# Layer 0 of a convolution and attention kernel: other weights for sharing out the depthwise taps, and an iteration's end written out by hand

## Chip, cores and metric

The kernel runs on one core of a Trainium2 chip. The metric is the device time of one execution in microseconds (us); lower is better. PE is the matrix engine, DVE the vector engine, ACT the scalar engine, POOL the general engine, SP the engine that issues the DMAs.

## What is computed

Eight images of 256 channels and 32 x 32 positions go through two layers. The change is in layer 0, which is, for each image (`_ln` scales by the root mean square over the channels):

```python
a = _attention(_ln(x, norm1_w, norm1_b), ...)
x = x + gamma1 * a
f = _edffn(_ln(x, norm2_w, norm2_b), pi_w, dw_w, fft_p, po_w)
x = x + gamma2 * f

# _attention: 4 heads, 32 channels for q and k, 64 for v
qkv = _bn(_conv1x1(x, qkv_w), ...)
attn = softmax(einsum('bhkn,bhkm->bhnm', q, k) * SCALE)
out = einsum('bhdm,bhnm->bhdn', v, attn)
out = out + _bn(_dwconv3(v_img, pe_w), ...)      # a 3x3 depthwise convolution of v
return _bn(_conv1x1(out, proj_w), ...)

# _edffn
x = _dwconv3(_conv1x1(x, pi_w), dw_w)            # 1024 channels
x = gelu(x1) * x2                                # 512 channels
x = _conv1x1(x, po_w)
# then an 8x8 Fourier filter with fft_p
```

Layer 1 (causal attention over the eight images' tokens and a mixture of eight experts) is the same before and after.

## The kernel before

Layer 0 is a software pipeline over the images, one iteration `i` per image. `main_of(i)` (L1052) is a generator that issues, in one order, the work that is mostly PE's: the second norm of image i-1 (`norm2`) and the Fourier part of image i-2 (`spectrum`: `pz`, `pf`, `py`), woven with the first attention units; the rest of the attention of image i (`attend`, L725) woven with the queries and keys of image i+1 (`queries_keys`); and then the end: copies of the queries and keys into a stacked form (`stack`, 32 DMAs on SP), the values of image i+1 (`values`, L685), the last softmax denominators (`finish`, L809), the Gelus of image i-1 (`gelu_steps`), and the output projection with its residual (`project`, L815).

An attention unit is a block of 128 keys against 256 queries: four matmuls into `s`, an exponential on ACT (`pT`), and, one unit late, the products with the values (`po`) and with ones (`sums`). Eight units make a chunk of 256 queries, four chunks an image. After a chunk, `close` copies `po` and `sums` off (`pu`, `ss`), and some units later come a reciprocal on DVE (`sr`), its split in two on ACT and POOL (`rh`, `rl`), a spreading matmul (`rb`) and two DVE operations that add the chunk to `o`. For the last chunk of an image these steps are in `finish`.

The depthwise convolutions run on DVE, one multiply-add over 128 x 1024 elements for each tap (`tap`, L537): 16 taps for the values of image i (`v_conv`, into `o`), and 8 groups of 8 taps for the hidden channels of image i-1 (`hidden`, L886, into `x` or `conv`; the ninth tap is in ACT's eviction). Each group of `hidden` first needs a 1x1 convolution on PE, `ph`, in two halves, and two ACT evictions for each half, into `hpad` (padded, two buffers) and into the accumulator. `open_group` (L843) issues them at the fourth and the sixth tap of the group before. When a group of the second half of the channels and its Gelu are done, `gate` multiplies the two (`hid`, two DVE operations), and `spectrum` of the next iteration reads `hid`. At the fourth tap of the next to last group, `hidden` asks for one Gelu itself if none has been done.

Every generator yields a weight, an estimate in us. `together` (L411) issues the side generator (`hidden`, with `v_conv` as its lead) whenever its sum of weights is below that of the main one, and what is left at the main one's end is issued after it:

```python
    for us in main:
        a += us
        while side is not None and s < ratio * a:
            step = next(side, None)
```

All of this is program order: every engine works off its own queue in the order in which the instructions were issued, and waits on semaphores. Operations go through a wrapper that keeps this order, so in the profile they all have its line, L68, and are told apart by their tiles. `ps_s` (tag `s`) and `ps_m` (tag `mm`) are PSUM pools of two buffers each; `s`, the values' `pq`, `pz` and the first half of the projection use `ps_s`, and `ph`, the queries' `pq`, `tpv`, `rb` and the second half of the projection use `ps_m`.

An attention unit has the weight 1.75 (L803), and a tap of the lead its own 1.3 times 1.5 (L898). In the end, `values` and `project` have weights of their own, so taps are given out among them too; `finish` and the Gelus are put between the steps of `values`:

```python
ends = weave(finish(i), gelu_steps(i - 1) if i >= 1 else none(), 1)
if i + 1 < B:
    stack(i + 1)
    yield from weave(values(i + 1), ends, 1)
    yield from project(i, (0, 1))
```

Of the kernel before, what the change touches and what calls it, by code (L numbers as in the profile page):

```python
# [9 lines left out]
F32 = mybir.dt.float32  # L10
F32R = mybir.dt.float32r
BF16 = mybir.dt.bfloat16
AF = mybir.ActivationFunctionType
# [5 lines left out]
P = 128  # L19
B, C, H, W = 8, 256, 32, 32  # L20
N = H * W
HALF = 512
KC = C // P
# [50 lines left out]
def conv_attn_hybrid_kernel(  # L74
# [353 lines left out]
    with ExitStack() as l0:  # L428
# [101 lines left out]
        def interior(p, h):  # L530
            r = H // 2
            return p[:, 1 + h * r : 1 + (h + 1) * r, 1 : 1 + W]

        def rows(ap):
            return ap.rearrange("p (h w) -> p h w", w=W)
# [89 lines left out]
        def conv1x1(ps, w, o0, src, hs):  # L625
            for k in range(KC):
                pe.matmul(
                    ps, w[:, k, o0 : o0 + P], src[:, k, hs], start=(k == 0), stop=(k == KC - 1)
                )


        att = {}
# [52 lines left out]
        def values(b):  # L685


            vT = att[b]["vT"] = one.tile([P, NT, C], F32, tag="vT", name="vT")
            waiting = []

            def turn(g, h, full):
                tp = ps_m.tile([P, 4, P], F32, tag="mm", name="tpv")
                for j in range(4):
                    pe.transpose(tp[:, j, :], full[:, j * P : (j + 1) * P], ident)
                act.copy(vT[:, 4 * h : 4 * h + 4, g * P : (g + 1) * P], tp)

            for g in range(KC):
                bias = qkv_o[:, 2 + g : 3 + g]
                pq = ps_s.tile([P, 2, HALF], F32, tag="s", name="pq")
                for h in range(2):  # L700
                    hs = slice(h * HALF, (h + 1) * HALF)
                    conv1x1(pq[:, h, :], qkvw, (2 + g) * P, att[b]["xn"], hs)
                for h in range(2):
                    full = one.tile([P, HALF], F32, tag="full", name="vfull", bufs=2)
                    act.activation(full, pq[:, h, :], AF.Identity, bias=bias)
                    act.activation(interior(vpad[g], h), rows(pq[:, h, :]), AF.Identity, bias=bias)
                    yield 1.7
                    if waiting:
                        turn(*waiting.pop())
                        yield 0.5  # L710
                    waiting.append((g, h, full))
            turn(*waiting.pop())
            yield 0.5

        def v_conv(b):
            o = att[b]["o"] = one.tile([P, KC, N], F32, tag="o", name="o")
# [8 lines left out]
        def attend(b):  # L725

            qst, kst, vT = (att[b][n] for n in ("qst", "kst", "vT"))
            nj = NT  # L730
            todo = []

            def product(po, sm, j, pT):


                for pair in range(NH // 2):
                    for i in range(4):
                        ch = pair * P + i * KD
                        pe.matmul(
                            po[i * KD : (i + 1) * KD, pair, :],  # L740
                            vT[:, j, ch : ch + KD],
                            pT[:, ch // HD, :],
                            start=(j == 0 and pair == 0),
                            stop=(j == nj - 1 and pair == 1),
                        )
                for hd in range(NH):
                    pe.matmul(
                        sm[hd * KD : (hd + 1) * KD, :], ones[:, :KD], pT[:, hd, :], start=(j == 0), stop=(j == nj - 1)
                    )

            def close(c, po, sm):
                pu = two.tile([P, NH // 2, QC], F32, tag="pu", name="pu", bufs=1)
                act.copy(pu, po)
                ss = two.tile([P, QC], F32, tag="ss", name="ss", bufs=1)
                act.activation(ss, sm, AF.Copy, accum_out=accs[:, 0, b, c : c + 1])
                r = two.tile([P, QC], F32, tag="sr", name="sr", bufs=1)
                rh = two.tile([P, QC], F32R, tag="rh", name="rh", bufs=1)
                rl = two.tile([P, QC], F32R, tag="rl", name="rl", bufs=1)
                qs = slice(c * QC, (c + 1) * QC)

                def invert():
                    dve.reciprocal(r, ss)

                def split():
                    act.activation(rh, r, AF.Copy, accum_out=accs[:, 1, b, c : c + 1])
                    pool.tensor_sub(rl, r, rh.bitcast(F32))

                def spread():
                    rb = ps_m.tile([P, NH // 2, QC], F32, tag="mm", name="rb")
                    for pair in range(NH // 2):  # L770
                        pe.matmul(rb[:, pair, :], pick_r[:, pair, :], rh, start=True, stop=False)
                        pe.matmul(rb[:, pair, :], pick_r[:, pair, :], rl, start=False, stop=True)
                    o = att[b]["o"][:, :, qs]
                    dve.tensor_mul(pu, pu, rb)
                    dve.tensor_add(o, o, pu)

                return [None, invert, None, split, None, None, spread]

            def later():
                if todo:  # L780
                    step = todo.pop(0)
                    if step:
                        step()

            late = None
            for c in range(N // QC):
                qs = slice(c * QC, (c + 1) * QC)
                po = ps_o.tile([P, NH // 2, QC], F32, tag="po", name="po")
                sm = ps_o.tile([P, QC], F32, tag="sm", name="sums")
                for j in range(nj):  # L790
                    ks = slice(j * P, (j + 1) * P)
                    s = ps_s.tile([P, NH, QC], F32, tag="s", name="s")
                    for hd in range(NH):
                        pe.matmul(s[:, hd, :], kst[:, hd, ks], qst[:, hd, qs], start=True, stop=True)
                    pT = two.tile([P, NH, QC], F32, tag="pT", name="pT")
                    act.activation(pT, s, AF.Exp)
                    if late:
                        product(*late[:4])
                        if late[2] == nj - 1:
                            todo = close(c - 1, *late[:2])  # L800
                    late = (po, sm, j, pT)
                    later()
                    yield 1.75  # L803
            product(*late)
            todo = close(c, po, sm)
            att[b]["rest"] = todo
            yield 1.3

        def finish(b):  # L809
            for step in att[b]["rest"]:  # L810
                if step:
                    step()
                yield 0.4
# [72 lines left out]
        def hidden(b, lead, on_pe=(), alone=False):  # L886
# [4 lines left out]
            for i, us in enumerate(lead):  # L891
                if i == 14:
                    opening = open_group(b, 0, hpad[0])
                    cur = next(opening)
                if i in (14, 15):
                    next(opening)

                yield 1.5 * us  # L898
            if opening is None:
                opening = open_group(b, 0, hpad[0])  # L900
                cur = next(opening)
# [131 lines left out]
        def weave(main, side, every, rest=True):  # L1033

            for n, us in enumerate(main):
                yield us
                if n % every == every - 1:
                    step = next(side, None)
                    if step is not None:
                        yield step  # L1040
            if rest:
                yield from side

        def none():
            yield from ()

        def later_on(n, steps):
            for _ in range(n):
                yield 0.0
            yield from steps  # L1050

        def main_of(i):  # L1052

            steps = attend(i)
            if i >= 1:
                head = weave(norm2(i - 1), spectrum(i - 2) if i >= 2 else none(), 1)
                yield from weave(head, steps, 3, rest=False)  # L1060
            later = queries_keys(i + 1) if i + 1 < B else none()
            yield from weave(steps, later_on(2, weave(set_up(), later, 1) if i == 0 else later), 2)
            ends = weave(finish(i), gelu_steps(i - 1) if i >= 1 else none(), 1)
            if i + 1 < B:
                stack(i + 1)
                yield from weave(values(i + 1), ends, 1)
                yield from project(i, (0, 1))
            else:
                yield from weave(project(i, (0,)), ends, 1)
                yield from project(i, (1,))  # L1070


# [22 lines left out]
        nc.vector.tensor_mul(proj_o, proj_o, cols("gam1"))  # L1095
        for _ in steps:
            pass
        for _ in values(0):
            pass
        ng = HID // P  # L1100
        dw_w = cols("dw_w").rearrange("p (g k) -> p g k", k=9)
        pi_o = const.tile([P, 2 * ng], F32, name="pi_o")
# [445 lines left out]
    with ExitStack() as l2:  # L1548
# [235 lines left out]
        for n in range(len(pieces) + LAG3):  # L1784
            one_ = two_ = three = iter(())
            if n < len(pieces):
                h, b, e = pieces[n]
                i = n // NE
# [141 lines left out]
```

## Time and profile before

| | |
|---|---|
| median of 3 runs | 3302.47 us (3299.11 to 3310.37) |
| the profiled execution | 3301.58 us, span 3299.8 us |
| busy: PE, DVE, ACT, POOL | 3061.8 (93%), 2415.3 (73%), 1424.7 (43%), 308.4 (9%) us |
| attention units (`pT` on ACT, 256 of them) | from 46.3 to 1236.1 us, so layer 0 is roughly the first 1290 us |
| taps of the hidden channels and of the values | 1.28 to 1.30 us each |
| span of one iteration, images 2 to 6 | 160.8 us |

The profile is one execution; times in it count from its first instruction. A row of the timeline has the start, the time, the engine, the operation with its output and inputs, how many, and in brackets the idle time of that engine before it and what ended it. A 32-bit matmul shows as two records (`pp` x16 are eight instructions). A row of the table of windows has a stretch, its length, the busy time and the instructions of each engine in it, and the clock that PE was granted (PEclk, 1.00 is full).

### The profile page before, as it was taken

The page shows a single profiled execution, that of the slowest core. Times are in us where ns is not written, and L with a number is a line of the kernel's source. Part 1 is how long each engine was busy: PE and PEld are TensorE (multiplying, and loading weights), DVE is VectorE, ACT ScalarE, POOL GpSimd, SP SyncE. Part 2 cuts the span into 40 slices and gives each one's busy share as a digit, 9 for nine tenths or more (in the row PEclk, how much of TensorE's full clock was granted, in tenths as well). Part 3 has the DMA queues.
Part 4 walks back from the last instruction along what each step waited for, and adds up shares of the span by engine and source line. Part 5 has one row for each costly group of instructions (what it writes and reads, how often), then busy time and mean ns, then how long its engine had stood idle before and what let it go on. Part 6 is the DMA issues. An engine that isn't in the chain of part 4 may idle for free.

```text
span 3299.8 us, 43136 instructions
## 1 busy us (share of the span) xinstructions
PE 3061.8 (93%) x17218; PEld 2058.1 (62%) x17218; DVE 2415.3 (73%) x3796; ACT 1424.7 (43%) x2215; POOL 308.4 (9%) x472
## 2 busy tenths in 40 slices
PE   8997999999999996769999998999999999999999
PEld 4553555555555553346565665677878777777787
DVE  4378787878787876835555444588888878888887
ACT  4454455555555552323333332344444444444443
POOL 2100211111111100011222211000000000000000
PEclk9998999999999998889999999899999999999999
DMA  3202020202020200030111101200000000000000
GB/s 110 52 2 51 27 52 27 52 27 52 27 52 27 52 19 2 16 135 26 63 63 53 39 26 52 94 20 20 20 20 20 24 22 26 20 20 26 20 7 13
DMA packets 49831, 121.45 MB, mean 37 GB/s; under 512 B 7302, under 2 KB 20054, under 8 KB 45782
## 3 DMA queue, kind: packets, MB, share of 16 engines
q1 hardware_dynamic: 49622, 118.61, 11.4%
q8 instruction: 137, 2.24, 0.3%
q14 instruction: 72, 0.59, 0.1%
HBM read 48.20 MB, written 37.88 MB: 26 GB/s over the span
## 4 chain that ended last, share of the span: by engine, by line
PE 48%; DVE 5%; ACT 1%; POOL 1%; issue 1%; DMA 0%; SPq 0%; POOLq 0%; ACTq 0%; DVEq 0%
PE pm L68 12%; PE pa L68 12%; PE q L68 11%; PE s L68 4%; PE po L68 3%; PE pv L68 2%; PE pk L68 2%; DVE nm L68 1%; DVE pr L68 1%; DVE zt L68 1%; DVE st L68 1%; ACT pr L68 1%; PE tp L68 1%; DVE h L68 1%; PE tpz L68 1%
## 5 line engine op out<-in xcount | busy, mean ns | idle before, releaser
L68 ACT ACTIVATE h<-h,bn_o,bn_s 128x512 f32<-128x512 f32 x384 | 308.6, 813 | 628.5 <-DVE h L68 628.4
L68 DVE SCALAR_TENSOR_TENSOR conv<-hpad,vec,conv 128x1024 f32<-128x1024 f32 x256 | 330.5, 1296 | 14.1 <-ACT conv L68 8.3
L68 DVE SCALAR_TENSOR_TENSOR x<-hpad,vec,x 128x1024 f32<-128x1024 f32 x248 | 320.0, 1295 | 26.3 <-ACT x L68 20.5
L68 PE MATMUL pm<-h,w 128*128 128x512 f32 (+1 forms) x768 | 323.4, 530 | 0.0
L68 ACT ACTIVATE pT<-s 128x1024 f32<-128x1024 f32 x256 | 261.4, 1023 | 135.2 <-PE s L68 134.5
L68 PE MATMUL po<-pT,vT 128*32 128x256 f32 x4096 | 276.4, 388 | 6.9 <-ACT pT L68 6.4
L68 PE MATMUL ph<-xn,piw 128*128 128x512 f32 x512 | 250.2, 617 | 6.9 <-DVE t L68 3.9
L68 PE MATMUL s<-kk,z 128*128 128x512 f32 x512 | 244.7, 606 | 0.6 <-DVE pr L68 0.6
L68 PE MATMUL s<-qst,kst 128*128 128x256 f32 x1024 | 212.5, 330 | 0.0
L68 PEld LDWEIGHTS s<-qst,kst 128*128 128x128 f32 x1024 | 145.6, 191 | 87.4 <-issue 81.2
L68 PEld LDWEIGHTS pm<-h,w 128*128 128x128 f32 x768 | 147.7, 192 | 77.1 <-issue 63.4
L68 ACT ACTIVATE hpad<-ph,pi_o 128x512 f32<-128x512 f32 x126 | 87.1, 691 | 250.0 <-PE ph L68 225.8
L68 DVE TENSOR_TENSOR h<-pa,first 128x512 f32<-128x512 f32 x128 | 88.3, 690 | 138.2 <-PE pa L68 136.5
L68 DVE TENSOR_TENSOR h<-h,wb 128x1024 f32<-128x1024 f32 x128 | 156.3, 1221 | 41.0 <-ACT h L68 41.0
L68 PE MATMUL pz<-pow__117,hid 128*128 128x256 f32 x512 | 131.3, 410 | 55.7 <-DVE hid L68 55.7
L68 DVE SCALAR_TENSOR_TENSOR o<-vpad,pe_w,o 128x1024 f32<-128x1024 f32 x128 | 163.3, 1280 | 14.5 <-ACT o L68 11.6
L68 DVE TENSOR_TENSOR h<-h,first 128x256 f32<-128x256 f32 x384 | 163.2, 425 | 13.2
L68 PEld LDWEIGHTS po<-pT,vT 128*32 128x32 f32 x4096 | 107.4, 109 | 90.8 <-ACT pT L68 8.1
L68 PEld LDWEIGHTS ph<-xn,piw 128*128 128x128 f32 x512 | 91.1, 192 | 116.2 <-issue 92.8
L68 PE MATMUL pa<-tz,ws 128*128 128x256 f32 x512 | 156.1, 387 | 3.0 <-DMA ws<-sums_d 3.0
L68 PE MATMUL sums<-pT,ones 128*32 128x256 f32 x2048 | 158.8, 382 | 0.0
L68 PE MATMUL q<-t,ws 128*128 128x256 f32 x512 | 152.7, 380 | 0.8 <-DVE t L68 0.8
(279 smaller groups left out, 5853.6 us busy)
## 6 DMA issues: line engine op xcount, KB each, us to landing
td<-t SPq DMA_DIRECT2D x8, 1024.0 KB, 3.8
t<-td SPq DMA_DIRECT2D x8, 1024.0 KB, 4.8
te<-ud SPq DMA_DIRECT2D x16, 512.0 KB, 3.9
out_dram<-te SPq DMA_DIRECT2D x16, 512.0 KB, 2.8
ze<-zd SPq DMA_DIRECT2D x15, 512.0 KB, 3.9
t<-in_x_dram SPq DMA_DIRECT2D x7, 1024.0 KB, 6.3
qst<-hi SPq DMA_DIRECT2D x56, 128.0 KB, 2.3
qst<-lo SPq DMA_DIRECT2D x56, 128.0 KB, 2.3
```

Source lines behind the costliest of these rows:

```text
L68: return self._tc.keep_in_program_order(method(*args, **kwargs))
```

## The change

An attention unit has the weight 2.4 and a tap of the lead 1.3 times 1.7. The end of all iterations but the last is a new generator, `ending`, whose steps have no weight, so that no tap is issued between them. Its order is: first half of the values' matmuls (`product(0)`), the reciprocal of the last chunk, a Gelu, evictions (`take(0)`), the second half's matmuls, the split of the reciprocal, a Gelu, the transposes of the first half (`turn`), the first half of the projection, the evictions of the second half, a Gelu, the spreading of the reciprocals, the second transposes, and the second half of the projection. `values` returns its three pieces for this in place of being a generator; before the first iteration they are called in the order product, take, turn, turn. The last iteration keeps its end, and its calls are the same.

```diff
@@ values @@
-            waiting = []
-
-            def turn(g, h, full):
+            pqs, fulls = {}, {}
+
+            def product(g):
+                pq = pqs[g] = ps_s.tile([P, 2, HALF], F32, tag="s", name="pq")
+                for h in range(2):
+                    conv1x1(pq[:, h, :], qkvw, (2 + g) * P, att[b]["xn"], slice(h * HALF, (h + 1) * HALF))
+
+            def take(g):
+                bias = qkv_o[:, 2 + g : 3 + g]
+                for h in range(2):
+                    full = fulls[g, h] = one.tile([P, HALF], F32, tag="full", name="vfull", bufs=2)
+                    act.activation(full, pqs[g][:, h, :], AF.Identity, bias=bias)
+                    act.activation(interior(vpad[g], h), rows(pqs[g][:, h, :]), AF.Identity, bias=bias)
+
+            def turn(g, h):
                 tp = ps_m.tile([P, 4, P], F32, tag="mm", name="tpv")
+                full = fulls.pop((g, h))
...
+            return product, take, turn
@@ attend @@
-                    yield 1.75
+                    yield 2.4
@@ hidden @@
-                yield 1.5 * us
+                yield 1.7 * us
@@ new @@
+        def ending(i):
+            product, take, turn = values(i + 1)
+            gelus = gelu_steps(i - 1) if i >= 1 else none()
+            rest = finish(i)
+            product(0)
+            yield 0.0
+            next(rest)
+            next(rest)
+            next(gelus, None)
+            take(0)
+            product(1)
+            yield 0.0
+            next(rest)
+            next(rest)
+            next(gelus, None)
+            for h in range(2):
+                turn(0, h)
+                yield 0.0
+            for _ in project(i, (0,)):
+                yield 0.0
+            take(1)
+            next(gelus, None)
+            for _ in rest:
+                pass
+            for h in range(2):
+                turn(1, h)
+                yield 0.0
+            for _ in gelus:
+                pass
+            for _ in project(i, (1,)):
+                yield 0.0
@@ main_of @@
-            ends = weave(finish(i), gelu_steps(i - 1) if i >= 1 else none(), 1)
             if i + 1 < B:
                 stack(i + 1)
-                yield from weave(values(i + 1), ends, 1)
-                yield from project(i, (0, 1))
+                yield from ending(i)
             else:
-                yield from weave(project(i, (0,)), ends, 1)
+                yield from weave(project(i, (0,)), weave(finish(i), gelu_steps(i - 1), 1), 1)
                 yield from project(i, (1,))
@@ before the loop @@
-        for _ in values(0):
-            pass
+        product, take, turn = values(0)
+        for g in range(KC):
+            product(g)
+            take(g)
+            for h in range(2):
+                turn(g, h)
```

More of the change, by code (lines that the diff above doesn't have):

```diff
@@ L695, in turn @@
                 act.copy(vT[:, 4 * h : 4 * h + 4, g * P : (g + 1) * P], tp)
[L697 to L713, printed above, removed]
+            return product, take, turn
         def v_conv(b):
```

## The prediction

> **What bounds the kernel now.** I read the page first (PE is busy for 93% of the span, and the longest pieces of the chain of waits are PE matmuls), then the table of windows. The change touches only layer 0, the first 1290 us. There, images 2 to 6 repeat every 160.8 us, so I cut one of these iterations (image 5) into its first part, its attention part and its end, and add the ends of images 7, 1 and 0:
>
> ```profile
> core 0: us, PE busy (x) PEld busy (x) DVE busy (x) ACT busy (x) POOL busy (x), PEclk, DMA share, GB/s
> 799.80:844.10 44.30, 42.74 (x298) 28.48 (x298) 38.60 (x44) 19.80 (x29) 8.84 (x14) 1.00 0.01 1
> 844.10:932.80 88.70, 85.81 (x857) 46.70 (x855) 70.98 (x62) 50.94 (x78) 14.01 (x17) 1.00 0.10 33
> 932.80:960.60 27.80, 23.37 (x61) 11.09 (x62) 25.10 (x25) 15.65 (x26) 0.84 (x1) 0.88 0.54 124
> 1237.60:1287.50 49.90, 24.12 (x60) 11.85 (x60) 42.90 (x42) 12.76 (x20) 1.06 (x1) 0.73 0.01 2
> 262.60:292.50 29.90, 25.45 (x72) 11.77 (x68) 24.70 (x24) 18.23 (x30) 0.93 (x1) 0.94 0.57 130
> 292.50:321.40 28.90, 11.06 (x28) 6.18 (x32) 28.29 (x27) 6.01 (x8) 0.00 (x0) 0.70 0.00 0
> 131.00:153.00 22.00, 19.15 (x81) 8.93 (x84) 6.05 (x8) 10.18 (x21) 0.72 (x1) 1.00 0.76 175
> ```
>
> The attention part is PE's: 85.8 of 88.7 us, while DVE is idle for 17.7. In the end it is the reverse: DVE 25.1 of 27.8, PE waiting, and its granted clock at 0.88. The last image is the extreme: 49.9 us with PE busy for half. Next, the timeline of PE in that end of image 5, and of its `pp` in image 0's end for comparison (start, us, engine, what, idle before):
>
> ```profile
> 944.57 0.66 PE L68 MATMUL tpv<-ident,vfull 128*128 128x128 f32 x4 [0.40 <-ACT vfull L68]
> 947.15 0.65 PE L68 MATMUL tpv<-ident,vfull 128*128 128x128 f32 x4 [1.93 <-ACT vfull L68]
> 949.56 0.58 PE L68 MATMUL rb<-rh,pick_r 128*128 128x256 f32 x1 [1.75 <-ACT rh L68]
> 951.29 9.33 PE L68 MATMUL pp<-o,projw 128*128 128x512 f32 x16
> ```
> ```profile
> 145.93 7.03 PE L68 MATMUL pp<-o,projw 128*128 128x512 f32 x16
> ```
>
> Two waits of 1.9 and 1.75 us, and then a projection of 9.33 us that takes 7.03 elsewhere (part of the 2.3 may be its second half's wait for `o`). Last, what DVE waits for in the attention part (total, times, longest):
>
> ```profile
> DVE pu L68 <- PE rb L68: 5.3, 2, 4.1
> DVE xn L68 <- PE rbn L68: 4.4, 1, 4.4
> DVE lo L68 <- ACT hi L68: 4.2, 2, 3.3
> DVE sr L68 <- ACT ss L68: 2.0, 2, 1.3
> ```
>
> DVE is ahead there: its taps have been given out too thinly for the time PE takes, and it stands at the next result of PE or ACT.
>
> [...] 0.88 in the end, after 3.7 us of idling within 4.9 us, and 1.00 in the attention part with gaps up to 1.1; (1-0.88) of 27.8 us is 3.3 us of PE's clock lost. [...] the `sr` of the end stands behind every tap given out before it (944.6, twelve us after `sums`). [...] The trace has 1.28 us, with the Gelu 0.01 us behind it; I use 1.28.
>
> **The change part by part.** *How many taps move.* Weights up to the start of the end, images 2 to 6: attention 32x1.75+1.3 = 57.3, `norm2` 6.4, `spectrum` 21.2, `queries_keys` 13.2, sum 98.1. The first 16 taps cost 1.3x1.5 = 1.95 each, the other 64 1.3, so 68 of 80 are given out and 12 are left (the window shows 14, DVE being two behind). Now attention is 78.1, the sum 118.9, and the taps cost 16x2.21+64x1.3 = 118.6: none is left. Image 1 (no `spectrum`) reaches 97.7, that is 64 taps instead of 52; image 7 (no `queries_keys`) 71 instead of 58. So the change doesn't do what it says in images 1 and 7, where 16 and 2 taps still come behind the projection.
>
> *Attention part, images 2 to 6.* 14 taps at 1.30 us (18.22 us in the window) come in: DVE 70.98+18.2 = 89.2 us. With them come two halves of `ph` at 1.72 = 3.4 us of PE. The first Gelu moves into attention, because the next to last group asks for one at its fourth tap: the order on ACT shows a table load, the Gelu, two half groups' evictions, and a table load back before the next `pT`. The pair of loads and the Gelu is 2x1.28+1.06 = 3.6 us of ACT; PE has 5.2 us of `ph` and `pq` beside it but only two `mm` buffers, so `pT` and with it `po` come late by between 0 and 3.6; taken 2.0. One us more for further half groups ahead of a `pT` (0 to 2; today's waits of this kind are 0.8 to 1.1 each). PE: 88.7+3.4+2.0+1.0 = 95.1. DVE has 89.2 of work in it, so 5.9 us may be lost to the waits above instead of 17.7; DVE may also run some three taps late before a `hpad` write on ACT stops, which is why I take it as covered.
>
> *The end.* From the end of `sums`, by the order listed and the durations of the trace. PE: `pq` 3.4+3.4, eight `tpv` to 8.0, first half of `pp` 3.5 to 11.5, `rb` 0.6 to 12.1, four `tpv` to 12.6. ACT: `pu`, `ss`, table, Gelu to 3.5; the first four evictions 3.7 to 6.0; `rh`, Gelu to 7.6; `vT` to 8.9; four evictions to 11.2; Gelu to 12.2. So the first `tpv`, `pp` and `rb` wait for nothing. DVE has no tap: `t` of the first half to 12.4, `hid` to 13.7, `pu` and `o` to 15.1. PE's last `tpv` need the buffer that `pu` frees (14.5), the second half of `pp` needs `o`: 15.3 to 18.8. I take 19.2 for 27.8, at full clock, the longest gap being 1.9. Bounds: 17.7 (no gap) and 22.5 (3.3 us of half clock come back).
>
> *First part.* The 0.7 us that `pz` waits for the last `hid` goes: 43.6 for 44.3. SP's queue: the 32 copies of `stack` take 20.2 us and 2.3 to land from the last `s` on; the next `s` comes some 26 us after that instead of 37, still behind them. POOL has one `rl`. Hidden, at nothing.
>
> Per image: 43.6+95.1+19.2 = 157.9 against 160.8, -2.9; five images -14.5.
>
> *Image 7.* Attention part +6.9 (four halves of `ph`), +2 (tables), +0.5. Then DVE: today 36.7 us of its 42.9 behind `sums` are taps (31.5) and gates; now nine taps (11.8), the gates (5.2), `sr`, `pu`, `o` and `t` (5.9) make 23 us, and with some 4 of waits for Gelu and projection the last `hid` is about 27 us after `sums`, not 46.4. Sum 9.4+27-46.4 = -10 (-5 to -13). *Image 1:* 109.6+6.9+1 in its first part, 19.5 for 29.9, then 16 taps, gates and `pz` 29.5 for 28.9, since PE has nothing else: -2. *Image 0:* its end, without Gelus, is 20.1 today: -1. *Prologue:* the second `pq` now waits behind `tpv` that wait for ACT: +1. Each of these three may be 3 off to either side.
>
> Sum: -14.5-10-2-1+1 = -26.5. The profiled execution took 3301.6 (span 3299.8 and 1.8 around it), 0.9 under the median; so about 3275 there, and **3276** as a median.
>
> **Rivals.** (a) *The clock returns, nothing is gained.* If the gap before the second `pp` pushes PE to half clock in each end as now (3.3 us lost), and the table loads cost all of their 3.6 us, the five images give 5x(-2.9+3.3+1.6) = +10 in place of -14.5, so 3300. For it: today's ends fall to half clock on gaps of this size. Against: today two of them stand in a row, and the end as worked out has one. (b) *DVE becomes the bound, slower.* In the attention part DVE's 89.2 us meet a window of 95.1. It decides from 5.9 us of DVE waits on. If the 15.9 us listed above all stayed, an image would take 10.0 more: 5x(-2.9+10.0) = +35.5, less 12 in the other images: about 3326. For it: DVE at 94%, and every late `xn`, `lo`, `pu` holds a `pq` or `mm` buffer. Against: these waits come from being ahead, and an engine with more work is less ahead. (c) *More is gained:* no cost for tables and evictions, 5x(-5.9), image 7 at -13: 3258.
>
> **How the numbers follow.** Forecast 0.62 (3264 to 3291), (a) and what lies between 0.20, (b) 0.15, (c) 0.03. A measurement of this kernel tells 0.3% (10 us) from no change. Faster 0.65, same 0.20, slower 0.15. The range, 3256 to 3308, leaves out (b) and a little of both sides.
>
> **What would show it.** Right: image 5's period near 158; its end under 20 with PE's clock at 1.00 and no tap in it; `pp` in two runs of 3.5; DVE's waits in attention under 6 us; two more table loads per image, PE waiting some 2 us for `pT` behind them; image 7's last `hid` some 27 us after `sums`. Wrong: new PE waits for `xn`, `lo` or `pu`, ACT's `hpad` waiting for DVE, or half clock in the ends.

## The result and the profile after

The changed kernel takes 3280.08 us (3277.43 to 3281.69, four runs), the kernel before beside it 3302.87 (3299.11 to 3310.37): a ratio of 0.9931 [0.9918, 0.9945]. The profiled execution took 3277.43 us, its span is 3275.3. The forecast was 3276, so the total came out almost as written. That it did is luck: the five middle images, which were to bring 14.5 us, lost 0.9, and other parts, some of them not touched by the change, brought more than was forecast of them.

The table of windows of the changed kernel, cut as it was for the kernel before: image 5's first part, attention part and end; the tail of image 7 from its last `sums` to its norm's first matmul; image 1's end; the drain behind image 1's projection; image 0's end.

```profile
core 0: us, PE busy (x) PEld busy (x) DVE busy (x) ACT busy (x) POOL busy (x), PEclk, DMA share, GB/s
796.80:841.80 45.00, 43.03 (x299) 28.67 (x298) 36.35 (x39) 18.64 (x27) 8.38 (x14) 1.00 0.01 1
841.80:936.40 94.60, 89.58 (x864) 47.87 (x862) 85.69 (x74) 56.73 (x85) 17.01 (x17) 1.00 0.10 31
936.40:957.20 20.80, 18.26 (x57) 9.14 (x54) 13.38 (x17) 13.38 (x23) 1.11 (x1) 0.92 0.74 167
1243.20:1269.30 26.10, 15.76 (x43) 8.44 (x39) 21.67 (x25) 6.43 (x11) 1.11 (x1) 0.80 0.00 0
...
269.80:287.80 18.00, 16.74 (x57) 8.56 (x54) 7.52 (x9) 13.25 (x22) 0.73 (x1) 1.00 0.87 198
287.80:317.10 29.30, 9.77 (x24) 5.62 (x23) 28.57 (x26) 6.01 (x8) 0.00 (x0) 0.65 0.03 7
131.60:150.60 19.00, 17.75 (x76) 8.69 (x72) 5.96 (x8) 9.75 (x21) 0.72 (x1) 1.00 0.85 194
```

The work moved as intended. The attention part of an image holds 14.7 us more DVE work (85.69 for 70.98), the end 11.7 us less. But the three lengths sum to 160.4 where they summed to 160.8: the end gave 7.0 back, the attention part took 5.9, and the first part 0.7. PE's clock in the end is 0.92, not 1.00.

The timeline of PE in that end shows why:

```profile
944.30 3.60 PE L68 MATMUL pp<-o,projw 128*128 128x512 f32 x8
...
949.49 0.66 PE L68 MATMUL tpv<-ident,vfull 128*128 128x128 f32 x4 [0.68 <-ACT vT L68]
952.01 5.23 PE L68 MATMUL pp<-o,projw 128*128 128x512 f32 x8 [1.87 <-DVE o L68]
```

The projection is in two runs, and the first takes 3.60 us at full clock (PEclk 1.00 from 944.3 to 947.9). The second, the same eight instructions, takes 5.23: the clock granted is 0.50 from 952.0 to 954.5. Ahead of it, between 948.8 and 952.0, PE does 0.66 us of transposes and nothing else.

The waits of DVE in the attention part (total, times, longest) answer to the four of before, 15.9 us there and 7.5 here:

```profile
DVE pu L68 <- PE rb L68: 4.1, 2, 2.9
DVE lo L68 <- ACT hi L68: 2.5, 2, 2.3
DVE sr L68 <- ACT ss L68: 0.5, 1, 0.5
DVE x L68 <- ACT x L68: 0.4, 1, 0.4
```

And the waits of PE in the same stretch:

```profile
PE ph L68 <- ACT conv L68: 2.8, 1, 2.8
PE po L68 <- ACT pT L68: 1.2, 1, 1.2
PE tr L68 <- ACT conv L68: 1.0, 1, 1.0
```

The first two are behind the Gelu that now lies in the attention part. The timeline there, of ACT, DVE and PE:

```profile
911.98 5.46 DVE L68 SCALAR_TENSOR_TENSOR conv<-hpad,vec,conv 128x1024 f32<-128x1024 f32 x4
...
913.15 1.28 ACT L68 ACT_TABLE_LOAD   x1
...
914.44 1.06 ACT L68 ACTIVATE x<-x 128x1024 f32<-128x1024 f32 x1
...
915.41 0.68 ACT L68 ACTIVATE hpad<-ph,pi_o 128x512 f32<-128x512 f32 x1
...
917.36 1.28 DVE L68 TENSOR_TENSOR hid<-x,conv 128x512 f32<-128x512 f32 x2
...
918.68 0.78 ACT L68 ACTIVATE conv<-ph,dw_o,vec 128x512 f32<-128x512 f32 x1 [2.60 <-DVE hid L68]
...
919.51 1.98 PE L68 MATMUL ph<-xn,piw 128*128 128x512 f32 x4 [2.83 <-ACT conv L68]
...
922.90 1.28 ACT L68 ACT_TABLE_LOAD   x1
...
925.27 1.07 PE L68 MATMUL po<-pT,vT 128*32 128x256 f32 x16 [1.21 <-ACT pT L68]
```

Read it from the bracket of 918.68: ACT wants to write a new accumulator `conv`, a pool of three, whose oldest buffer is read by the gate `hid`. DVE does that gate only at 917.36, behind the four taps queued ahead of it (from 911.98), though the Gelu that the gate reads is done at 915.50. ACT stands for 2.60 us, the `mm` buffer that its eviction frees comes late, and `ph` stands for 2.83.

### The profile page after: what moved, and what is told of

Same layout as the page of the kernel before. It is cut to its first block, busy times and chain, and to the rows that moved or that the text cites. A ratio compares the mean times of both kernels' runs of the same rounds, so it can differ in the third digit from the quotient of the medians.

```text
span 3275.3 us, 43158 instructions
## 1 busy us (share of the span) xinstructions
PE 3047.3 (93%) x17218; PEld 2050.7 (63%) x17218; DVE 2417.4 (74%) x3796; ACT 1438.2 (44%) x2227; POOL 327.9 (10%) x472
## 4 chain that ended last, share of the span: by engine, by line
PE 48%; DVE 6%; ACT 1%; issue 1%; POOL 1%; DMA 0%; SPq 0%; ACTq 0%; POOLq 0%; DVEq 0%
PE pm L68 13%; PE pa L68 12%; PE q L68 12%; PE s L68 4%; PE po L68 3%; PE pv L68 2%; PE pk L68 2%; DVE nm L68 1%; DVE pr L68 1%; DVE zt L68 1%; DVE st L68 1%; ACT pr L68 1%; PE tp L68 1%; PE tpz L68 1%; PE tpt L68 1%
## 5 line engine op out<-in xcount | busy, mean ns | idle before, releaser
L68 DVE SCALAR_TENSOR_TENSOR conv<-hpad,vec,conv 128x1024 f32<-128x1024 f32 x256 | 331.5, 1301 | 14.3 <-ACT conv L68 8.4
L68 ACT ACTIVATE pT<-s 128x1024 f32<-128x1024 f32 x256 | 261.5, 1024 | 128.1 <-PE s L68 127.0
L68 DVE TENSOR_TENSOR h<-h,wb 128x1024 f32<-128x1024 f32 x128 | 156.2, 1221 | 41.0 <-ACT h L68 41.0
L68 DVE SCALAR_TENSOR_TENSOR o<-vpad,pe_w,o 128x1024 f32<-128x1024 f32 x128 | 163.6, 1283 | 17.4 <-ACT o L68 14.7
```

The source lines that it names most:

```text
L68: return self._tc.keep_in_program_order(method(*args, **kwargs))
```

## Where the 24.5 us of span came from

By the ends of the projections in both traces: image 0 -2.4; image 1 -2.3; image 2 +2.7 (counted so, the drain behind image 1's projection, 0.4 longer, falls into it; and in it the late gate's wait, read above in image 5, was also followed by half clock: PEclk 0.57 from 436 to 440 us); images 3 to 6 together -1.8; image 7, up to its norm's first matmul, -14.3. That makes -18.1. The rest of layer 0 and layer 1, whose instructions are untouched, add -3.1 and -3.3, together -6.4.

## Experiments

Theory: the weights cure image 7 and nothing else by themselves; the new order of the end gains, and loses part again because the second half of the projection waits for `o`; what the attention part pays is a late gate, not the table loads. Rivals: the order of the end is what gains; the table loads and ACT's extra evictions are what costs; or DVE, now busy for 91% of the attention part, simply binds. All runs have the kernel before beside them (3302.05, 3302.75 and 3304.35 us in the three groups, in the order told).

### The weights alone, with the old end

```diff
 # before.py
-                    yield 1.75
+                    yield 2.4
-                yield 1.5 * us
+                yield 1.7 * us
```

> The two weights (2.4 and 1.7) with the end of the kernel before. Theory (the weights move the taps; that is what image 7 gains by, and the end written out by hand is needed for images 2 to 6): image 7 falls from 166.0 to about 152 us as in the changed kernel, while the end of image 5, in the old order but without a tap, takes 22 to 23 us (20.8 in the changed kernel, 27.8 before), so images 2 to 6 come to 161.5 to 162.5 each, no better than the 160.8 of before. Time 3288 to 3296. Rival (the new order of the end does nothing, the absence of taps from it everything): the end of image 5 is 20.8 us here too and the time 3280.

Measured: 3297.60 us (3293.82 to 3301.63), ratio 0.9985 [0.9978, 0.9991]; 1.6 us above the expected range. Images 3 to 6 take 165.3 each, 4.4 more than before (160.9 by the ends of the projections). Image 7 takes 151.6, the same as with the new end. Image 5's end without taps, by the windows (columns as above) and by PE's timeline:

```profile
947.10:971.40 24.30, 19.23 (x53) 9.34 (x53) 13.21 (x16) 12.94 (x23) 0.95 (x1) 0.86 0.62 141
```
```profile
959.05 1.12 PE L68 MATMUL tpv<-ident,vfull 128*128 128x128 f32 x4 [1.93 <-ACT vfull L68]
961.45 0.58 PE L68 MATMUL rb<-rh,pick_r 128*128 128x256 f32 x1 [1.29 <-ACT rh L68]
...
963.28 8.13 PE L68 MATMUL pp<-o,projw 128*128 128x512 f32 x16
```

Taking the taps out shortens the old end by 3.5 us only: both waits on ACT and the half clock remain (PEclk 0.95 in this end, and 8.13 us of `pp` where image 0's end took 7.03 before). They weren't caused by the taps. So the whole gain of image 7 belongs to the weights, and for images 3 to 6 the weights alone are a loss; the order of the end pays for them. Up to image 7's norm this trace is 1.7 us behind that of the kernel before (1289.2 for 1287.4): the little that the weights alone gain in all comes from behind it, where nothing was changed.

### The new end alone, with the old weights

```diff
 # after.py
-                    yield 2.4
+                    yield 1.75
-                yield 1.7 * us
+                yield 1.5 * us
```

> The new end with the old weights (1.75 and 1.5). Theory: 12 taps of each of the images 2 to 6 are then left behind the projection, and the next image's first matmul waits for the last gate: 12 x 1.3 us plus two gates, about 17 us, in which PE has nearly nothing, against 3.4 us less in the attention part: 8 to 11 us more in each of five images, image 1 with 28 taps left some 12 us more, image 7 as before the change. Time 3340 to 3365. Rival (the order of the end is what gains, the weights do little): 3280 to 3300.

Measured: 3356.13 us (3354.87 to 3358.45), ratio 1.0165 [1.0149, 1.018]; a period of 170.7, 9.8 more. The taps that are given out neither in the attention part nor in the end are issued behind the projection, and `pz` of the next first part waits 15.3 us for `hid`:

```profile
817.20:879.50 62.30, 46.06 (x301) 30.11 (x300) 53.47 (x55) 20.91 (x31) 8.39 (x14) 0.89 0.00 1
```

62.3 us for 44.3. In layer 0 neither part gains without the other.

### The spreading of the reciprocals ahead of the projection

```diff
             for h in range(2):
                 turn(0, h)
                 yield 0.0
+            for _ in rest:
+                pass
             for _ in project(i, (0,)):
                 yield 0.0
             take(1)
             next(gelus, None)
-            for _ in rest:
-                pass
```

> The changed kernel with the spreading of the last reciprocals moved ahead of the first half of the projection. Theory (the 1.87 us that PE waits for o ahead of the second half, and the 1.7 us of half clock behind it, are what makes the end 20.8 us and not 19.2 or less): rb comes right behind the transposes, o is ready while PE does the first half, the wait and the half clock go, and the end of image 5 is 17.3 to 18.3 us; seven images gain 2 to 3.5 each, 3256 to 3266. Rival (the wait only moves: PE waits for rl, then for the copies of the second transposes, and the clock falls as before): the end stays at 20 to 21 us and the time at 3277 to 3282.

Measured: 3263.25 us (3262.34 to 3264.42), ratio 0.9881 [0.9866, 0.9896], 16.8 under the changed kernel; a period of 156.9. The end in the windows, and PE's timeline in it:

```profile
922.40:939.60 17.20, 16.70 (x57) 8.48 (x54) 13.29 (x17) 13.20 (x23) 1.11 (x1) 1.00 0.87 199
```
```profile
930.63 0.39 PE L68 MATMUL rb<-rh,pick_r 128*128 128x256 f32 x1 [0.26 <-ACT vT L68]
...
931.21 3.60 PE L68 MATMUL pp<-o,projw 128*128 128x512 f32 x8
...
935.92 3.70 PE L68 MATMUL pp<-o,projw 128*128 128x512 f32 x8 [0.24 <-ACT vT L68]
```

DVE now finishes `o` under the first half of the projection. Both gaps go, the second half takes 3.70 us for 5.23, and the clock stays at 1.00. The end falls from 20.8 to 17.2: 2.05 of it are waits (0.50 left of 2.55), 1.53 the half clock. So the wait for `o`, with the half clock behind it, was the fault of the end, and with it gone the end is below the predicted lower bound of 17.7. Up to image 7's norm, where the change lies, the gain is larger than in the total: 21.1 us (1248.2 for 1269.3). The unchanged rest happened to take 8.0 us more in this trace (see the last section).

### The first Gelu one group earlier

```diff
-                            if m + 2 == len(on_dve) and not hid["gelu"]:
+                            if m + 3 == len(on_dve) and not hid["gelu"]:
```

> The changed kernel with the first Gelu asked for one group (8 taps) earlier. Theory (of the 4.0 us that PE waits behind it in image 5, the 2.8 on ph come because ACT can't evict into the last group's tile until DVE has done the gate, and DVE is late; the 1.2 on pT are the table loads): one group earlier the gate is long done when that tile is wanted, ACT does not wait for DVE, and 2.5 to 3 us of each of the images 2 to 7 go; image 1 gets the pair of loads in its attention too and loses 1 to 2. Time 3263 to 3268. Rival (the two table loads and the Gelu make the whole wait, wherever they stand): the 4.0 us stay, time 3277 to 3283.

Measured: 3263.12 us (3261.58 to 3265.36), ratio 0.9882 [0.9867, 0.9897], 17.0 under the changed kernel. The attention part in the windows, and all that PE waits for in it:

```profile
830.60:921.00 90.40, 89.42 (x865) 47.94 (x863) 84.00 (x73) 56.97 (x85) 16.97 (x17) 1.00 0.10 33
```
```profile
PE tr L68 <- ACT conv L68: 1.0, 1, 1.0
```

94.6 us became 90.4. The two table loads and the Gelu are still there, only eight taps earlier, and PE waits for them nowhere; the gate is done before its accumulator is wanted. So the 2.8 us were the late gate's. The 1.2 on `pT` went with them; since the run moves the loads together with the gate, it shows that a pair of loads need not cost PE anything, not that their share in the 1.2 was nothing at the old place. The end gave 1.0 back (21.8 us), since this run keeps the wait for `o`.

### A lead factor of 1.6

```diff
-                yield 1.7 * us
+                yield 1.6 * us
```

> The changed kernel with a lead weight of 1.6 in place of 1.7. Theory: the first part of an iteration is 45.0 us and not 44.3 as before because the taps of the values are given out more sparsely, and the first two ph of the hidden groups so stand one behind the other with ACT's eviction between them (PE waits 0.59 and 0.56 us for it); with 1.6 one of the two waits or both go, 0.5 to 1.1 us in six images: time 3273 to 3279. Rival (the two waits come with the larger weight of an attention unit, not with the lead): the first part stays at 45.0 and the time at 3278 to 3283.

Measured: 3257.70 us (3256.79 to 3259.01), ratio 0.9867 [0.9852, 0.9882]. Theory and rival both missed, by 15 us and more. The first part is unchanged (45.1 us), so this step of the lead's weight does not shorten it; it is the attention part that fell, to 91.4. The waits of PE and of ACT there:

```profile
PE pq L68 <- ACT conv L68: 1.2, 1, 1.2
PE po L68 <- ACT pT L68: 0.9, 1, 0.9
```
```profile
ACT conv L68 <- DVE hid L68: 3.4, 1, 3.4
```

ACT's wait for the gate is longer than in the changed kernel (3.4 for 2.6), and PE waits 2.1 us in all, for 5.0 there. With the taps given out at other places the wait probably falls where PE has more other work at hand; no run shows that apart. Its length alone, at any rate, doesn't tell what it costs.

### More work for DVE

One operation of DVE behind two taps of each hidden group; the values stay the same.

```diff
                     tap(dst, pad, dw_w[:, n, :], k)
+                    if i in (1, 5) and not alone:
+                        dve.tensor_scalar_mul(dst, dst, 1.0)
```

> The changed kernel with a multiplication by 1.0 of the accumulator (128 x 1024) put behind two of the eight taps of each hidden group: 16 more DVE operations per image and some 12 of them in its attention part. Theory (rival b of the prediction is a matter of amount: DVE has 85.7 us of work in 94.6 of the attention part, so about 9 us of room, part of it behind waits): [...] DVE waits for nothing there and each of the images 2 to 6 grows by 4 to 9 us, image 1 by the operations of its drained groups too; 3310 to 3345. Rival (PE is the bound with room to spare, or DVE's lag is absorbed in the end without taps): at most 2 us per image, under 3296.

Measured: 3321.94 us (3319.91 to 3325.03), ratio 1.0062 [1.0047, 1.0078]; a period of 167.3. In the attention part 9.2 us of DVE work cost 6.2 (100.8 for 94.6), hardly through `lo` or `xn` (1.0 us of new waits), but in the main at the same place as above:

```profile
PE ph L68 <- ACT conv L68: 5.8, 1, 5.8
```
```profile
ACT conv L68 <- DVE hid L68: 5.0, 1, 5.0
```

Of the 6.2 us, 3.4 are more waiting of PE, and 2.8 are more busy time of PE for the same work, at half clock behind that wait (PEclk 0.97 in this part, 1.00 in the changed kernel). So DVE has some 3 us of room there, all told, and what goes beyond reaches PE through ACT's queue.

### A larger share of taps in image 1

```diff
-                together(main_of(i), hidden(i - 1, v_conv(i)), SIDE)
+                together(main_of(i), hidden(i - 1, v_conv(i)), 1.22 if i == 1 else SIDE)
```

> The changed kernel with the side given out 1.22 times as fast in image 1 alone, so that all of its taps are out before the end (the weights of its main part are 97.7, of the side 118.6). Theory (the 29.3 us behind image 1's projection are 16 taps and two gates on DVE with PE waiting at half clock): the drain goes, and image 1's part up to the end grows by the 16 taps at most, since DVE becomes the bound there (98.4 us of work in 119.2, plus 21): from the end of image 0's projection to the first s of image 2 some 148 to 156 us, not 167.1. Time 3262 to 3272. Rival (DVE as the bound makes PE wait as long in attention as it waited in the drain): 3276 to 3283.

Measured: 3269.69 us (3265.18 to 3274.81), ratio 0.9907 [0.9892, 0.9922]. From the end of image 0's projection to image 2's first `s` it takes 155.6 us for 167.2: the drain of 29.3 us behind image 1's projection, with PE's clock at 0.65, is gone, against new waits of PE in its attention part, 5.0 for `conv` and 2.1 for `lo`.

### Together

The earlier spreading with the earlier Gelu:

> The changed kernel with the spreading moved ahead of the projection's first half and the first Gelu asked for one group earlier, that is both of the gains found. Theory (the two waits are in different places and independent): images 2 to 6 at 157.0 - 3.5 = 153 to 154 us each, time 3244 to 3251. Rival (the gains overlap, since DVE then sets the pace of the attention part): 155.5 to 157 us, 3256 to 3262.

Measured: 3247.39 us (3244.82 to 3249.39), ratio 0.9834 [0.982, 0.9847]: by the totals the 16.8 and 17.0 add up, to 32.7. By the images they don't: images 3 to 6 gain 3.5 and 3.2 us each alone and 5.1 together, and up to image 7's norm it is 21.1 and 18.7 alone and 30.3 together. That the totals add up is due to the unchanged rest of the kernel, which differs from trace to trace. The images alternate between 154.5 and 156.2 instead of the expected 153 to 154. The end has a wait again, of 2.15 us in all five, and in images 2, 4 and 6 PE's half clock comes behind it (5.29 us of `pp` for 3.60). Images 3, 4 and 5:

```profile
612.49 0.39 PE L68 MATMUL rb<-rh,pick_r 128*128 128x256 f32 x1 [2.15 <-ACT vT L68]
...
613.07 3.60 PE L68 MATMUL pp<-o,projw 128*128 128x512 f32 x8
...
766.95 0.39 PE L68 MATMUL rb<-rh,pick_r 128*128 128x256 f32 x1 [2.15 <-ACT vT L68]
...
767.53 5.29 PE L68 MATMUL pp<-o,projw 128*128 128x512 f32 x8
...
923.11 0.39 PE L68 MATMUL rb<-rh,pick_r 128*128 128x256 f32 x1 [2.15 <-ACT vT L68]
```

With the lead factor of 1.6 added, and a ratio of 1.2 in image 1:

> All gains found in one: the spreading ahead of the projection's first half, the first Gelu a group earlier, a lead weight of 1.6, and the side given out 1.2 times as fast in image 1. Theory (they sit in different places): images 2 to 6 at 153 to 155 us, image 1 some 11 us shorter than in the kernel with the first two alone (3247.4): 3231 to 3240. Rival (the lead weight gains only by moving ACT's wait for the first gate away from PE, which the earlier Gelu has done already, and image 1's drain comes back as waits): 3244 to 3250.

Measured: 3222.94 us (3220.82 to 3226.37), ratio 0.9755 [0.9739, 0.9772], 8 us below the expected range; images 2 to 6 take 152.0.

Then also the second Gelu of the end behind the first transposes, so that ACT copies `vT` ahead of it:

```diff
             next(rest)
             next(rest)
-            next(gelus, None)
             for h in range(2):
                 turn(0, h)
                 yield 0.0
+            next(gelus, None)
             for _ in rest:
                 pass
```

> The kernel of best1 with the second Gelu of the end behind the copies of the first transposes. Theory (with the Gelu a group earlier the end has a new wait: rb needs the buffer that ACT frees with those copies, and they stand behind that Gelu, 2.15 us in image 5, and half clock in every other image): the wait falls below 0.6, 1.2 to 2.5 us in five or six images, 6 to 13 us under best1. Rival (DVE's gates come later by as much and the projection waits for pu and o instead): within 3 us of best1.

Measured: **3213.37 us (3209.74 to 3216.50), ratio 0.9724 [0.9707, 0.9741]**, the best version, which beats both kernels. The windows of image 5, first part, attention part, end:

```profile
753.00:798.00 45.00, 42.72 (x297) 28.66 (x296) 37.17 (x38) 19.31 (x28) 9.42 (x14) 1.00 0.01 1
798.00:887.50 89.50, 89.17 (x866) 47.98 (x864) 84.57 (x75) 56.24 (x85) 17.69 (x17) 1.00 0.11 34
887.50:904.60 17.10, 16.62 (x53) 8.39 (x54) 13.47 (x17) 13.26 (x23) 1.11 (x1) 1.00 0.87 197
```

The attention part and the end are PE's, but for 0.3 and 0.5 us. The step from 3222.94 to 3213.37 lies in the expected 6 to 13 us and is still not the expected mechanism: the earlier changes had already cut the wait to 0.6 us, so an image gains only 0.35. In the two profiles (spans 3220.5 and 3211.5) 2.3 us of the difference lie up to the end of image 7's projection, and 6.7 behind it, where the instructions are the same.

## Why the prediction was right, point by point

- **What bounds each part: right.** PE in the attention part, DVE with PE waiting in the old end and in image 7. The run with the weights alone corrects one reading: the waits of PE in the old end were ACT's order more than DVE's taps, since they stayed when the taps went.
- **Which taps move: right.** None is given out in image 5's end (the four that lie there are DVE being late), and image 1 still has 16 behind its projection, whose drain took 29.3 us for the predicted 29.5.
- **The attention part: right in sum, 94.6 for 95.1, and wrong in its cause.** PE is busy for 3.8 us more (3.4 predicted) and waits 2.1 more, where the terms of 2.0 for the tables and 1.0 for further evictions stood: 4.0 of new waits came, and 1.9 of the old ones went. The earlier Gelu shows that 2.8 of the 4.0 came from the gate being late, and not from the loads. A sign that the prediction named against itself came in another form: ACT does wait for DVE, at `conv` for `hid` and not at `hpad`.
- **The end: 20.8 for 19.2.** One gap of 1.87 came where 1.9 was named as the longest, but in another place: it was worked out for the last `tpv`, as a wait for `pu`. These `tpv` ran ahead of `pu` (949.49, and `pu` at 950.46), after 0.68 of waiting for `vT`, and the 1.87 came behind them, as the wait of the second `pp` for `o`. The sum put the half clock at nothing because no gap was longer than 1.9. That a gap of this size leaves the clock alone was the author's estimate, and the trace shows otherwise: behind the two waits there, 0.68 and 1.87 us, the half clock came back, at some 1.5 us (`pp` 5.23 us for 3.70 in the run with the earlier spreading). Rival (a) was half right: one of its two costs came, at half its price.
- **The first part: 45.0 for 43.6.** This step failed outright. It was to lose 0.7 and gained 0.7. The wait of `pz` for `hid` did go, but PE has two new waits of 1.1 us together for `ph`, behind ACT's eviction into `x`; with a lead factor of 1.6 these became one of 1.65 for `ph`, behind DVE, and the length stayed. So what sets it is still open.
- **Images 2 to 6, the main term: -14.5 predicted, +0.9 measured.** The first part is 1.4 off, the end 1.6, the attention part 0.5 the other way: 2.5 of the 2.9 per image. So images 3 to 6 gain 0.4 each, and image 2, with its half clock at 436 us, turns that into a small loss. The total hid this: the main term was missed by 15.4 us, and image 7, image 0 and what lies behind came out 13.4 better than forecast. That they did so by nearly as much is luck.
- **Image 7: -14.3 for -10.** The mis-sized term is the one behind `sums`: the last `hid` ends 22.6 us after it, not 27. The 4 us put down for waits of DVE weren't there; it was busy for 21.67 of 26.1.
- **Image 0 with the prologue: -2.4, image 1: -2.3**, for nothing (-1 and +1) and -2.
- **Behind layer 0's images: -6.4, for nothing.** This was no part of the sum, and it made up for part of the missed main term.
- **Rival (b), DVE as the bound: not reached.** Its waits fell from 15.9 to 7.5 us, short of the predicted under 6. The run with more DVE work shows how near it is: about 3 us. Its path is in the main not the one that the rival named (`xn`, `lo`, `pu`), but the accumulator pool and ACT.

## What to carry to other kernels

When work is moved off one stage, cost the stage that takes it by the buffers that the moved work holds, not by engine time alone: here a shared pool of three let a late DVE stop ACT, and ACT stop PE, while both had time to spare. When the order of a stage is written by hand, put what starts a chain over several engines (spread, multiply, add, then the matmul that needs it) a full block of independent matmuls ahead of its consumer; that alone was worth 16.8 us in the total. And a total that comes out right says little about its terms: compare stage by stage before believing the reasons, and the unchanged stages too.

## What the runs showed of the hardware

- **Half clock came behind some gaps of PE, and the length of a single gap does not tell which.** In the changed kernel the wait of 1.87 to 1.88 us ahead of the second `pp`, with one of 0.68 us just before it, was followed by half clock in all of images 2 to 6 (`pp` took 5.22 to 5.30 us; in the earlier spreading, with 0.24 us of waiting, 3.70). The longer wait of 2.82 to 2.84 us for the late gate was not followed by it in images 3 to 6 (the `ph` behind it took 1.98 us, with PEclk 1.00) and was in image 2 (3.58 us). In the run of the two together the wait ahead of `rb` was 2.15 to 2.16 us in all five images, and half clock came behind it in images 2, 4 and 6 (`pp` 5.29 us) and not in 3 and 5 (3.60 us). No run shows what decides it.
- **Unchanged instructions took up to 11 us more or less.** What lies behind image 7's norm is the same in all twelve kernels, and takes from 2003.5 to 2014.2 us in their traces (2012.4 before, 2006.0 after). From layer 1's first `nm` to its last it takes 566.3 us before and 564.3 after, with the same 64 instructions, and the offset between the two traces changes in steps of some 1.4 to 1.7 us, at stretches of half clock that the other trace doesn't have (PEclk 0.50 from 1853.0 to 1856.0 after, where the same instructions before, from 1874 to 1877, had 1.00; 0.50 from 1949.0 to 1952.0 before, where after, from 1927.5 to 1930.5, they had 1.00). No run shows why they fall where they do. It is the size of what a change of this kernel can be credited with by mistake.
- **A table load took 1.28 us, and the Gelu behind it did not wait further.** In image 5 of the changed kernel the load runs from 913.15 to 914.43 us and the Gelu starts at 914.44. With the earlier Gelu a pair of loads in the attention part cost PE nothing that shows: of 90.4 us there PE waited 1.0, at `tr` for ACT's `conv`.
- **The added multiplication was shorter than a tap.** The `tensor_scalar_mul` over 128 x 1024 elements took 0.69 to 0.77 us on average; a tap over as many took 1.28 to 1.30 in the traces of both kernels.
